# The square of a projection: read from PSUM, or from the copy in SBUF

## Chip, core and metric

The kernel runs on one core of one Trainium2 chip. The metric is the device time of one execution in microseconds (us). Engines: PE is TensorE (PEld its weight loads), DVE is VectorE, ACT is ScalarE, POOL is GpSimd, SP is SyncE, which only issues DMAs. "L303" is line 303 of the kernel.

## What is computed

The reference takes x of shape 4 x 512 x 128 and adds to it, in turn: half of a gated mixture of eight experts, a linear attention, the mixture again, half of a six-layer network, an attention with two key sets, and half of the six-layer network again. The change lies in the six-layer network, which therefore runs twice, 12 layers in all. The part of one layer that matters:

```python
q = l2norm(q) * qs
k = l2norm(k) * ksc
q = q * cos * scale + rotate_half(q) * sin * scale
k = k * cos * inv + rotate_half(k) * sin * inv
out = local_attention(q, k, v)      # 16 heads of 64, windows of 32, scores times 8, softmax
x = x + out @ Wo
x = x + ffn_layer(shift_tokens(x))  # layer norm, product gated by gelu
```

`l2norm` divides each head's vector by its length, so the sum of the squares of every k and q vector is needed. All of it is float32.

## The kernel before

**Units.** A layer is cut into 8 units: 4 batch rows b of 512 tokens, times 2 halves hf of 8 heads. A unit has 8 projections c (0 to 3 for k, 4 to 7 for q), each a 128 x 512 tile, features on the partitions. Over 12 layers these are 96 units and 768 projections.

**One projection** (`proj`) has five steps:
1. PE multiplies x with the weights in three passes (L274 to L276) into a PSUM bank `ps`, in the profile `qkps`, one of four banks that are shared with most other matmuls.
2. ACT copies it to SBUF, into a quarter of the tile `raw` (L300).
3. ACT squares it into `sq` (L303). PE sums the squares of the heads into `n2` (L321 for k, L355 for q).
4. DVE multiplies `ps` with the cosine table into `rtk` or `rtq` (L308).
5. POOL multiplies `raw` in place with the sine table (L310).

When four projections are through, `swap` (L389) issues two DMAs from POOL's queue that add the exchanged rows of `raw` onto `rtk` or `rtq`: this is the rotation.

**Lengths.** `norm` and `norm_q` turn the sums into reciprocal square roots with small operations of DVE (k: L327, L328, L335 to L342; q: L360, L362, L370 to L372) and of ACT (k: L330, L331, L345; q: L365, L366). For k, PE spreads them over the tile (`R`, L380) and DVE multiplies them in (L383). For q they enter the softmax.

**Attention.** `score` is PE (L419 the mask, L428). `soft` is DVE's maximum (L438) and difference (L440), POOL's product (L443), ACT's Exp (L445), DVE's sum (L448) and reciprocal (L450), POOL's product (L452) and DVE's transpose (L455). `vproj` (L401, copied by ACT at L407) gives values already multiplied with Wo, `out` (L471) and `add` (L478) put the result on x.

**Feed-forward**, once for each b and layer, in `Ffn`: two DMAs on SP's queue fetch the shifted half of x into `xs` (L601, L602); statistics on DVE (L607 to L612, L620 to L622), normalised on POOL (L626 to L628), gate, Gelu (L660, with two table loads), product (L671), output (L677).

**Order.** In the two runs of the six-layer network the order of instructions on each engine is written out: every step has a time in a table (`TIMES`), is held behind the steps that it needs, and all steps are sorted by that time and issued in this order. Each engine works through its own queue in order; waits between engines are put in by the framework from what each instruction reads and writes. In that order the square stands behind the copy and before DVE's product, and all steps of neighbouring units are interleaved. The preparation of weights (L182, L184 for the projections, L194 for the tables) and of x (`make_xT`, L259 to L269) lies among them.

The lines around the change:

```python
        nc.scalar.copy(raw, ps)
        yield
        self.sqs[c] = sq = tile_of(g, "t2", [128, 512], F32, "sq")
        nc.scalar.activation(sq, ps, AF.Square)
        yield
```

Of the kernel before, what the change touches and what calls it, by code (L numbers as in the profile page):

```python
# [9 lines left out]
AF = mybir.ActivationFunctionType  # L10
# [44 lines left out]
def tile_of(g, tag, shape, dt=F32, name=None, bufs=1):  # L55

    n = math.prod(shape[1:])
    e = 2 if dt == BF else 4
    size, bufs = SIZES.get(tag, (n * e, bufs))
    t = g.mem.tile([128, size // e], dt, tag=tag, name=name or tag, bufs=bufs)[0:shape[0], 0:n]  # L60
    if len(shape) > 2:
        d = "abcd"[:len(shape) - 1]
        t = t.rearrange("p (%s) -> p %s" % (" ".join(d), " ".join(d)), **dict(zip(d[1:], shape[2:])))
    return t
# [6 lines left out]
def bank(g, tag, shape=(128, 512), name=None):  # L71
    n = math.prod(shape[1:])
    t = g.psum.tile([128, 1024 if tag == "S" else 512], F32, tag=tag, name=name or tag, bufs=BANKS[tag])[0:shape[0], 0:n]
    if len(shape) > 2:
        d = "abcd"[:len(shape) - 1]
        t = t.rearrange("p (%s) -> p %s" % (" ".join(d), " ".join(d)), **dict(zip(d[1:], shape[2:])))
    return t
# [195 lines left out]
def mm3(nc, out, wh, wl, xh, xl):  # L273
    nc.tensor.matmul(out, lhsT=wh, rhs=xh, start=True, stop=False)  # L274
    nc.tensor.matmul(out, lhsT=wh, rhs=xl, start=False, stop=False)  # L275
    nc.tensor.matmul(out, lhsT=wl, rhs=xh, start=False, stop=True)  # L276


class Unit:
# [8 lines left out]
    def proj(self, c):  # L288
        g = self.g
        nc = g.nc  # L290
        xT = g.xT[(self.l, self.b)]
        s, i = c // 4, c % 4
        ps = bank(g, "mm", [128, 512], "qkps")
        W = g.wqk[(self.l, self.hf, c)]
        mm3(nc, ps, W[:, 0, :], W[:, 1, :], xT[:, 0, 0:512], xT[:, 1, 0:512])
        yield
        if i == 0:
            self.raw[s] = tile_of(g, "raw", [128, 4, 512], F32, "raw")
        raw = self.raw[s][:, i, :]
        nc.scalar.copy(raw, ps)  # L300
        yield
        self.sqs[c] = sq = tile_of(g, "t2", [128, 512], F32, "sq")
        nc.scalar.activation(sq, ps, AF.Square)  # L303
        yield
        if i == 0:
            self.rt[s] = tile_of(g, ("rtk", "rtq")[s], [128, 4, 512], F32)
        rot = g.rot[(self.l, s)]
        nc.vector.tensor_tensor(self.rt[s][:, i, :], ps, rot[:, 0, :], ALU.mult)  # L308
        yield
        nc.gpsimd.tensor_tensor(raw, raw, rot[:, 1, :], ALU.mult)  # L310
        yield
# [1047 lines left out]
```

## Time and profile before

| | |
|---|---|
| median of 3 runs | 4491.85 us (4482.15 to 4493.92) |
| the profiled execution's own time | 4486.91 us |
| its span, first to last instruction | 4485.1 us |
| mean granted TensorE clock | 0.939 |
| L300, copy, ACT | 768 times, 590 ns mean |
| L303, square, ACT | 768 times, 616 ns mean |
| L308, product with cosine, DVE | 768 times, 678 (k) and 684 ns (q) mean |
| L310, product with sine, POOL | 768 times, 1362 ns in the page's mean, median 1286 |
| swap (L389) | 384 DMAs of 512 KB, 6.5 to 6.7 us to landing |

Time is in us, the length of a single instruction in ns where marked. A group's line gives its busy time, the mean length of one, and the idle time of the engine just before it with what ended most of it. A line of the waits reads: who waited, for whom, total us, times, longest. The chain that ended last is followed back from the last instruction, at each step to what released it; its shares are of the span. In the timeline and the chain, times count from the start of the span.

### The profile page before, as it was taken

Reading aid. Unit: us, or ns where it says so; the run is one execution under the profiler, and the core shown is the slowest. Engines: PE = TensorE matmul, PEld = TensorE weight load, DVE = VectorE, ACT = ScalarE, POOL = GpSimd, SP = SyncE. Lnnn points to the kernel's source line nnn. Section 1 sums busy time; section 2 is a strip of 40 time slices with the busy share of each in tenths; the row PEclk is TensorE's granted clock in tenths of the full one; section 3 lists DMA queues with packets and bytes.
Section 4 is the critical chain, followed back from the end, with each engine's and each line's share of the span. In section 5 each row is a group of like instructions: output and inputs, shape, how many; then the busy total and the mean of one; then the engine's idle time right before and its main releaser. Section 6 shows DMA issues by size and latency. Waiting matters only on the chain.

```text
span 4485.1 us, 150251 instructions
## 1 busy us (share of the span) xinstructions
PE 3865.4 (86%) x66435; PEld 2663.9 (59%) x66436; DVE 3705.2 (83%) x6415; ACT 2604.5 (58%) x5050; POOL 2493.1 (56%) x2164
## 2 busy tenths in 40 slices
PE   8989978898888888988869998888889889888886
PEld 5666646666666666666533434566666666566665
DVE  6968978888898888888867776888888888888886
ACT  5434455665565565665536666555656656556563
POOL 4625656666666666666501112666666666666663
PEclk9999989999999999999979999999999999999998
DMA  2000033433434334343331222333343343433432
GB/s 61 19 10 15 22 86 74 90 70 81 88 66 91 71 76 88 70 88 73 84 95 49 69 76 52 70 80 82 72 86 73 78 90 61 89 69 77 85 62 49
DMA packets 163852, 312.44 MB, mean 70 GB/s; under 512 B 41304, under 2 KB 125664, under 8 KB 138176
## 3 DMA queue, kind: packets, MB, share of 16 engines
q0 software_dynamic: 31008, 202.40, 22.8%
q1 hardware_dynamic: 132192, 100.44, 7.8%
q8 instruction: 520, 8.52, 0.8%
q14 instruction: 132, 1.08, 0.1%
HBM read 77.49 MB, written 17.69 MB: 21 GB/s over the span
## 4 chain that ended last, share of the span: by engine, by line
DVE 38%; PE 37%; DMA 12%; issue 6%; ACT 4%; POOL 2%; SPq 1%; ACTq 0%; POOLq 0%; DVEq 0%
DMA xs<-x 10%; DVE sm L448 4%; PE vps L401 3%; DVE h L935 3%; DVE E L440 3%; PE S L428 3%; DVE mx L438 3%; DVE xT L269 3%; PE av L471 3%; DVE rtq L308 3%; PE S L1147 2%; DVE pt L455 2%; PE av L1184 2%; PE qkps L274 2%; PE ST L1176 2%
## 5 line engine op out<-in xcount | busy, mean ns | idle before, releaser
L310 POOL TENSOR_TENSOR raw<-raw,rot 128x512 f32<-128x512 f32 x768 | 1006.8, 1362 | 544.2 <-ACT raw L300 540.4
L300 ACT COPY raw<-qkps 128x512 f32<-128x512 f32 x768 | 453.3, 590 | 662.2 <-PE qkps L276 643.7
L401 PE MATMUL vps<-vo,xF 128*32 128x256 f32 x12288 | 751.6, 386 | 40.0 <-issue 29.3
L401 PEld LDWEIGHTS vps<-vo,xF 128*32 128x32 f32 x12288 | 405.9, 111 | 330.3 <-issue 81.6
L452 POOL TENSOR_TENSOR E<-E,smr 128x1024 f32<-128x1024 f32 x192 | 389.6, 2029 | 310.1 <-DVE smr L450 177.0
L407 ACT COPY vx<-vps 128x512 f32<-128x512 f32 x768 | 427.1, 584 | 108.6 <-PE vps L401 106.7
L303 ACT ACTIVATE sq<-qkps 128x512 f32<-128x512 f32 x768 | 473.1, 616 | 0.0
L443 POOL TENSOR_TENSOR E<-E,rq 128x1024 f32<-128x1024 f32 x192 | 388.8, 2025 | 95.6 <-DVE E L440 57.3
L471 PE MATMUL av<-vx,pt 128*32 128x128 f32 x11904 | 381.6, 275 | 58.1 <-DVE x L478 32.8
L274 PE MATMUL qkps<-xT,wqk 128*128 128x512 f32 x768 | 343.4, 447 | 73.3 <-DVE rtq L308 40.6
L471 PEld LDWEIGHTS av<-vx,pt 128*32 128x32 f32 x11904 | 335.7, 110 | 115.8 <-DVE x L478 49.3
L1148 DVE TENSOR_REDUCE nm<-S 128x1 f32<-128x512 f32 x512 | 325.2, 684 | 63.3 <-PE S L1147 62.7
L308 DVE TENSOR_TENSOR rtq<-qkps,rot 128x512 f32<-128x512 f32 x384 | 259.9, 684 | 134.2 <-ACT sq L303 132.6
L383 DVE TENSOR_TENSOR rtk<-rtk,R 128x512 f32<-128x512 f32 x384 | 254.0, 672 | 104.7 <-PE R L380 104.3
L677 PE MATMUL fout<-w,ge 128*128 128x128 f32 (+1 forms) x1152 | 231.9, 379 | 123.3 <-DVE rtk L383 120.4
L1177 ACT ACTIVATE E<-ST 128x512 f32<-128x512 f32 x512 | 273.8, 599 | 109.3 <-PE ST L1176 109.1
L937 POOL TENSOR_TENSOR h<-r,h 128x512 fp32r<-128x512 f32 x128 | 182.3, 1424 | 251.5 <-DVE h L935 237.9
L275 PE MATMUL qkps<-xT,wqk 128*128 128x512 f32 x768 | 310.9, 405 | 5.7 <-issue 2.9
L276 PE MATMUL qkps<-xT,wqk 128*128 128x512 f32 x768 | 309.4, 403 | 5.0 <-issue 5.0
L428 PE MATMUL S<-rtk,rtq 64*32 64x64 f32 (+1 forms) x24576 | 291.4, 229 | 15.5 <-issue 13.3
L428 PEld LDWEIGHTS S<-rtk,rtq 64*32 64x32 f32 x24576 | 284.1, 108 | 31.3 <-issue 18.1
L677 PEld LDWEIGHTS fout<-w,ge 128*128 128x128 f32 (+1 forms) x1152 | 218.4, 289 | 133.7 <-DVE rtk L383 129.4
(257 smaller groups left out, 8803.8 us busy)
## 6 DMA issues: line engine op xcount, KB each, us to landing
rtk<-raw POOLq DMA_DIRECT2D x192, 512.0 KB, 6.7
rtq<-raw POOLq DMA_DIRECT2D x192, 512.0 KB, 6.5
pd<-pc SPq DMA_DIRECT2D x36, 384.0 KB
wqkr<-in_L_ffn_Wqk SPq DMA_DIRECT2D x192, 64.0 KB
rot<-in_c_rot SPq DMA_DIRECT2D x24, 512.0 KB
k<-pd SPq DMA_DIRECT2D x32, 288.0 KB
r<-in_L_ffn_W SPq DMA_DIRECT2D x32, 256.0 KB
wvraw<-in_L_ffn_WvT SPq DMA_DIRECT2D x24, 256.0 KB
```

The costliest lines, as they stand in the source:

```text
L274: nc.tensor.matmul(out, lhsT=wh, rhs=xh, start=True, stop=False)
L300: nc.scalar.copy(raw, ps)
L303: nc.scalar.activation(sq, ps, AF.Square)
L308: nc.vector.tensor_tensor(self.rt[s][:, i, :], ps, rot[:, 0, :], ALU.mult)
L310: nc.gpsimd.tensor_tensor(raw, raw, rot[:, 1, :], ALU.mult)
L401: nc.tensor.matmul(ps[p * 32:(p + 1) * 32, ww, :], lhsT=xF[:, t0:t0 + 32], rhs=g.vo[(self.l, self.hf, p // 2)][:, p % 2, :], start=True, s ...
L407: nc.scalar.copy(self.v[th][:, 2 * t:2 * t + 2, :], ps)
L428: nc.tensor.matmul(self.S[k][p * 32:(p + 1) * 32, ab, w * 64 + 64 - n:w * 64 + 64], lhsT=self.rt[1][rows, p, t0:t0 + 32], rhs=self.rt[0][r ...
L443: nc.gpsimd.tensor_tensor(E4, E4, self.rq[:, :, 8 * k:8 * k + 8].unsqueeze(3).to_broadcast([128, 2, 8, 64]), ALU.mult)
L452: nc.gpsimd.tensor_tensor(E, E, r.unsqueeze(2).to_broadcast([128, 16, 64]), ALU.mult)
L471: g.nc.tensor.matmul(self.av[ww * 32:(ww + 1) * 32, k, :], lhsT=self.pt[w // 8][:, ab, w % 8, role, :], rhs=self.v[src // 8][:, src % 8, a ...
L677: nc.tensor.matmul(self.o[:, t, :], lhsT=h[0:k, t * 128:(t + 1) * 128], rhs=g.F[self.l].w2[0:k, i, :], start=(i == 0 and t == 0), stop=(i ...
```

## The change

The square's input is `raw`, the copy in SBUF, in place of `ps`, the bank in PSUM. Nothing else is touched: same engine, same size, same place in the order. The copy is written by the ACT instruction before it, and `raw` is later overwritten in place by L310.

```diff
         nc.scalar.copy(raw, ps)
         yield
         self.sqs[c] = sq = tile_of(g, "t2", [128, 512], F32, "sq")
-        nc.scalar.activation(sq, ps, AF.Square)
+        nc.scalar.activation(sq, raw, AF.Square)
         yield
```

## The prediction

> **What bounds the kernel.** I read the page first, for the busy shares and the chain that ended last; then the waits; then the users of the lines that the diff touches; then the chain and the timeline of a few stretches inside a feed-forward block.
>
> ```profile
> PE 3865.4 (86%) x66435; PEld 2663.9 (59%) x66436; DVE 3705.2 (83%) x6415; ACT 2604.5 (58%) x5050; POOL 2493.1 (56%) x2164
> ...
> DVE 38%; PE 37%; DMA 12%; issue 6%; ACT 4%; POOL 2%; SPq 1%; ACTq 0%; POOLq 0%; DVEq 0%
> ```
>
> No engine is full. The end is set by a chain that alternates between DVE and PE; ACT and POOL, which the diff loads, are 4% and 2% of it. So I ask what hangs on the changed line, L303, and on the POOL product L310 that overwrites the tile L303 will now read. From the list of waits, then from the view of L303 (who waited for it: total us, times):
>
> ```profile
> POOL raw L310 <- ACT raw L300: 540.4, 244, 24.4
> DVE rtq L308 <- ACT sq L303: 132.6, 153, 4.2
> DVE rtk L308 <- ACT sq L303: 29.6, 62, 4.1
> ```
>
> DVE's L308 waits 215 times for the square, whose result it does not use. Over all 768 projections L308 never starts sooner than 0.03 us after L303's end. Both read one PSUM bank, and the program orders them. POOL waits only for the copy, L300. One case, as the chain of waits tells it (start, us, what):
>
> ```profile
> 1061.88 0.59 ACT raw L300
> 1062.47 0.51 ACT sq L303
> 1063.00 0.69 DVE rtq L308
> 1063.69 1.14 DVE mx L438
> ```
>
> Copy, square, product, each released by the one before: 0.51 us of square stand in the chain. The timeline of the same stretch (start, us, engine, line; in brackets the idle time before) shows ACT and POOL:
>
> ```profile
> 1061.88 0.59 ACT L300 COPY raw<-qkps 128x512 f32<-128x512 f32 x1
> 1062.37 0.60 ACT L303 ACTIVATE sq<-qkps 128x512 f32<-128x512 f32 x1
> ...
> 1064.96 0.24 ACT L330 ACTIVATE ky<-kn 128x32 f32<-128x32 f32 x1
> 1065.23 0.23 ACT L331 ACTIVATE ky<-ky 128x32 f32<-128x32 f32 x1
> ```
>
> ```profile
> 1062.55 2.54 POOL L310 TENSOR_TENSOR raw<-raw,rot 128x512 f32<-128x512 f32 x2 [2.41 <-ACT raw L300]
> ```
>
> L303 starts 0.49 us after a copy that lasts 0.59: they overlap by 0.10. L331, which needs L330's result, starts 0.03 us after its end. L310 starts when the copy is through, beside the square.
>
> **Removed: DVE's wait for the square.** In 748 of 768 cases L303 follows L300 directly on ACT, and its end is 0.505 us after L300's (median). So L308 may start up to 0.505 us earlier. In the chain "ACT sq L303" has 83 pieces, 42.0 us. Of these 67 lead to L308; the rest to another copy (13) or other ACT work (3). For the 67 the gain is the smaller of 0.505 us and DVE's idle time before that L308: 30.4 us. How much is kept depends on what DVE waits for next. For 33 it is a POOL product that DVE itself releases (L452), or a sum on PE: 16.0 us, kept in full. For 24 it is PE's spread R (L380), which hangs on DVE as well as on ACT and PE: 9.7 us, between none and all; I take half, 4.9. For 10 it is the next square: 4.7 us, taken as lost. Sum -20.9; bounds -16.0 and -30.4. All 230 idle stretches of DVE before L308, cut in the same way, are 87.8 us; that is the limit if nothing but DVE counted.
>
> **Added on ACT.** L303 now needs L300's result: it starts about 0.03 us after L300's end (as L331 does) instead of 0.10 before it. Its length from SBUF is between its own 0.606 and 0.622 (the 128x512 cast from SBUF, L811, which takes 0.580 from PSUM); I take 0.62. Its end comes 0.65 us after L300's, not 0.505: +0.145 us, and over 748 pairs 108 us more of an engine that has 1880 us idle. On the path: 16 pieces of the chain where more ACT work follows, 2.3 us, and DVE's 30 waits for the Gelu (L671, 39.4 us), at most 4.4 us. Sum between +2.3 and +6.7; I take +4. The rest is covered by slack: the sum of the exponentials (L448) starts 1.18 us or more after its Exp ended in 95% of cases. A page differs a little here: the Trainium skill, "ScalarE: Activation LUTs", section "What ACT_TABLE_LOAD costs", gives back-to-back ACTIVATEs an overlap of 93 ns where these rows show 0.10 to 0.11 us; losing it would make the ACT sum 93 us (748 times 0.093 plus 0.031), an estimate from that page, against 108 from the rows.
>
> **Added on POOL.** L310 must not overwrite what the square still reads, so its release moves from L300's end to L303's, 0.65 us later. Behind it in POOL's queue stand the swap DMAs (L389), the two softmax products (L443, L452) and the layer norm (L626). Moving L310 alone and letting the queue's idle time absorb it, 572 of the 768 start later, by 0.54 us on average; 125 swaps by 0.30 (38 us), 56 of L443 by 0.29 (16 us), 23 of L626 by 0.53 (12 us), almost none of L452. I cost this at nothing, because: the q swap lands 4.6 us or more before the first score in 95% of cases, the k swap 21.8 us or more; L443 is followed by the Exp, whose slack is the 1.18 us above; L628 behind L626 waits for DVE in any case. Without that cover it is the 66 us just listed.
>
> **Moved: L310 against DVE's small operations.** From the timeline of DVE, and of POOL beside it:
>
> ```profile
> 1081.78 1.08 DVE L370 TENSOR_TENSOR qr<-qy 128x32 f32<-128x32 f32 x1
> 1082.89 1.19 DVE L371 SCALAR_TENSOR_TENSOR qr<-qr,qn 128x32 f32<-128x32 f32 x1
> 1084.12 0.19 DVE L372 SCALAR_TENSOR_TENSOR rq<-qr,qy 128x32 f32<-128x32 f32 x1
> ```
>
> ```profile
> 1081.54 2.49 POOL L310 TENSOR_TENSOR raw<-raw,rot 128x512 f32<-128x512 f32 x2 [1.13 <-ACT raw L300]
> ```
>
> L370 takes 0.18 us elsewhere. Here it begins 0.24 us after an L310 and ends with it, and L371 ends with the second. In the chain 96 pieces are held by an L310 in this way (L328, L184, L370, L371, L612), for 59.9 us. If each hold grew by the 0.54 us of L310's delay, this would be +52 us. If instead what comes first goes first, 38 of the 96 arrive before L310's new start and pass, 44 wait longer, and the net is -21.6 us; operations newly caught, mostly L372 and L184, give back 9 to 26. I take -4, the middle of -12 and +5, and keep +52 as the far end. The rule behind the milder reading: the Trainium skill, "SBUF — State Buffer", section "SBUF: two separate sides", has VectorE and GpSimd share a port pair as a lock that whichever starts first keeps for its whole instruction. It speaks against this change too, since a later L310 meets other DVE work; by it the term is the -4, by the plain reading of the rows the +52.
>
> **Sum.** -20.9 + 4 - 4 = -21 us. The profiled execution took 4486.91 us (span 4485.1 and 1.8 around it), 4.9 below the median of the three runs, 4491.85. The sum gives 4466 by the first and 4471 by the second; I give 4471, as a median is what will be compared.
>
> **Rivals.**
> - *L310, later, holds DVE longer (slower).* Place: L328, L184, L370, L371 and L612, in each of 48 block passes. Price: +52 - 20.9 + 4 = +35 us, 4527. It cancels the gain when the holds grow by 17 us in sum, and decides beyond. For it: 59.9 us of holds already in the chain, with L310 as holder. Against it: L370 arrives only 0.12 to 0.32 us after L310, less than the 0.54 by which L310 moves.
> - *The gain is absorbed (no change).* The chain holds 31 landings of xs, each 11 to 15 us; what DVE saves just before a landing is lost, and where the k swap (L389, 45 waits for L308) starts sooner it shares the DMA engines with xs: L602 lasts 6.14 us at its shortest and 7.13 as a rule, so up to 1 us for each of the 38 waits on xs. If half of these lost 1 us, +19 - 21: about 4490.
> - *The change doesn't do what it says:* L308 stays behind the square by another tie. Neither its inputs (the bank, rot) nor its output names one. Then only ACT's +4 to +7 and POOL's delay remain: 4495 to 4500.
> - *ACT becomes late everywhere.* +108 us in its queue, but with 42% idle and the slack above I keep it inside the range, not as a case.
>
> **How the numbers follow.** About 0.3%, 13.5 us, can be told from no change. Forecast 0.52 (0.48 of it faster by more than that, 0.04 within); held DVE 0.24 (0.22 slower, 0.02 within); absorbed 0.20 (0.12 within, 0.05 faster, 0.03 slower); not done 0.04 (0.03 slower, 0.01 within). Together 0.53, 0.19, 0.28. The forecast's own range is 4451 to 4480: from -30.4 - 12 + 2.3 to -16.0 + 4. The whole range begins lower, at 4440, since the runs before begin 10 us below their median, and reaches to 4505, over the absorbed case and a third of the held one.
>
> **What would show it.** Right: "DVE rtq L308 <- ACT sq L303" gone, replaced by shorter waits for L300; L303 starting just after L300's end, at 0.61 to 0.63 us; POOL's wait before L310 now for the square and longer; qr L370 below its mean of 0.71 us. Wrong: L328, L184 or L612 with longer means, more time in the chain under xs, or waits for Exp (L445) before L448.

## The result, and the profile after

The changed kernel takes 4522.98 us (median; 4515.39 to 4534.39), the kernel before 4487.03 us on the same chip (4477.91 to 4493.92): a ratio of 1.0085, 95% interval 1.0066 to 1.0104. It is slower, by some 36 us, where 21 us less was forecast; 4522.98 lies outside the range of 4440 to 4505. The profiled execution of the changed kernel took 4524.28 us, with a span of 4521.8 us (36.7 longer than before) and a mean granted TensorE clock of 0.928 (0.939 before).

The page of the changed kernel, engine totals and chain of the end:

```profile
PE 3881.4 (86%) x66435; PEld 2648.5 (59%) x66436; DVE 3625.8 (80%) x6415; ACT 2699.4 (60%) x5050; POOL 2491.8 (55%) x2164
...
DVE 38%; PE 32%; DMA 17%; issue 5%; ACT 5%; POOL 2%; SPq 0%; DVEq 0%; POOLq 0%; ACTq 0%
DMA xs<-x 15%; DVE sm L448 4%; PE vps L401 3%; DVE E L440 3%; DVE h L935 3%; DVE mx L438 3%; DVE xT L269 3%; DVE rtq L308 3%; PE S L1147 3%; DVE pt L455 3%; PE av L1184 3%; PE ST L1176 2%; PE S L428 2%; PE av L471 2%; PE qkps L274 2%
```

DVE was busy for 79 us less than before, and yet the end came later. In the chain the share of DMA went from 12% to 17%, all of the rise from the landing of `xs`, which was 10% of the span (427.6 us) and is 15% (678.8 us). The list of waits after the change (who waited for whom: total us, times, longest):

```profile
POOL raw L310 <- ACT sq L303: 596.9, 304, 25.0
...
DVE bst L609 <- DMA xs<-x: 305.2, 48, 9.2
...
DVE rtq L308 <- ACT raw L300: 78.9, 121, 4.2
```

and two lines of the same list of the kernel before:

```profile
POOL rtk L389 <- DVE rtk L308: 119.4, 45, 2.9
...
DVE bst L609 <- DMA xs<-x: 98.7, 38, 8.7
```

DVE's wait for the square is gone, and L308 now waits for the copy alone, as forecast. The new cost is in the second line: L609, the first statistics of the feed-forward block, waits for `xs` in all 48 passes, 305.2 us in place of 98.7. POOL's wait for L308 ahead of the k swap has nearly vanished (119.4 us before; 14.8 us, 11 times, after): the swap is issued sooner. The next step joins these two.

**One pass, after and before.** The timelines (start, length, engine, line; in brackets the idle time before). After:

```profile
1089.84 0.75 SPq L601 DMA_DIRECT2D xs<-x  x1
...
1090.29 0.18 DVE L370 TENSOR_TENSOR qr<-qy 128x32 f32<-128x32 f32 x1
1090.50 0.19 DVE L371 SCALAR_TENSOR_TENSOR qr<-qr,qn 128x32 f32<-128x32 f32 x1
...
1090.71 2.49 POOL L310 TENSOR_TENSOR raw<-raw,rot 128x512 f32<-128x512 f32 x2 [1.80 <-ACT sq L303]
1090.73 1.29 DVE L372 SCALAR_TENSOR_TENSOR rq<-qr,qy 128x32 f32<-128x32 f32 x1
...
1094.40 1.71 POOL L389 DMA_DIRECT2D rtk<-raw  x2 [1.20 <-DVE rtk L308]
...
1104.30 0.23 DVE L609 BATCH_NORM_STATS2 bst<-xs 128x6 f32<-128x64 f32 x1 [4.46 <-DMA xs<-x]
```

Before, the same place in the network (L310, L370 and L371 of this pass are shown in the prediction):

```profile
1081.34 0.75 SPq L601 DMA_DIRECT2D xs<-x  x1
...
1086.68 1.71 POOL L389 DMA_DIRECT2D rtk<-raw  x2 [2.65 <-DVE rtk L308]
...
1092.79 0.20 DVE L609 BATCH_NORM_STATS2 bst<-xs 128x6 f32<-128x64 f32 x1
```

Count from the issue of `xs` (L601). Before, L310 began at +0.20, just ahead of L370, and held L370 and L371 for 1.08 and 1.19 us. After, it begins at +0.87; L370 and L371 went through at 0.18 and 0.19 us, and only L372 is caught. DVE is that much sooner through its queue, so L308 of the last k projection is sooner done, and the k swap that waits for it is issued at +4.56 in place of +5.34. In most passes the swap comes sooner still (+3.87, below), as POOL then finds L308 already done. Then L609 starts at +14.46 in place of +11.45: DVE, which was ready sooner, waits 4.46 us for a transfer that lands 3 us later.

**Why the transfer lands later.** `xs` comes as 511 packets of 256 B on SP's queue (508 of L601, 3 of L602). The packet records of these two passes, and of the next pass of the changed kernel:

| start of packet, from the issue of `xs` | 100th | 450th | 490th | 495th | 500th | 508th |
|---|---|---|---|---|---|---|
| before | +3.13 | +8.10 | +8.66 | +8.74 | +8.80 | +8.92 |
| after | +3.14 | +8.11 | +8.67 | +9.94 | +12.51 | +13.89 |
| after, the next pass (swap at +3.87) | +3.61 | +13.52 | +14.08 | +14.15 | +14.22 | +14.34 |

In the first two rows nothing differs up to the 490th packet, at 71 in a us. The swap's packets, 8 KB and about 0.64 us each, begin at +6.8 before and at +6.0 after. They leave `xs` alone for more than 2 us; then `xs` all but stands, with single packets between theirs, until the swap's are through. Before, all but three packets of `xs` were through by then; after, some twenty were left.

The first pass shown after is one of ten of the milder kind, with the swap at +4.55 or +4.56. In 34 of the 46 passes it is issued at +3.86 to +3.93, as in the third row: there the standstill begins at about +8.0, after 386 to 440 packets, with 71 to 125 left. Either way ten packets get through in 5.1 us, and what is left then goes at the old rate. A pass that is caught so loses some 5 us, with twenty packets left or with a hundred.

**All passes.** In 46 passes (the last of each run of layers left out), medians, in us after the issue of `xs`, with the mean where it is used below:

| | k swap issued | DVE ready for L609 | first L609 (mean) | rest of the pass, mean | pass, mean |
|---|---|---|---|---|---|
| before | 5.54 | 12.19 | 13.60 (13.58) | 55.49 | 69.07 |
| after | 3.88 | 8.77 | 14.83 (14.83) | 54.96 | 69.79 |

Over the 48 passes the stretch from issue to L609 grew by 57.6 us in sum, and the rest shrank by 24.5; with 4.3 more ahead of the first pass this makes 37.4, close to the 36.7 us of the span.

### The profile page after: what moved, and what is told of

It is laid out like the page before. It is cut to its first block, busy times and chain, and to the rows that moved or that the text cites. A ratio compares the mean times of both kernels' runs of the same rounds, so it can differ in the third digit from the quotient of the medians.

```text
span 4521.8 us, 150253 instructions
## 1 busy us (share of the span) xinstructions
PE 3881.4 (86%) x66435; PEld 2648.5 (59%) x66436; DVE 3625.8 (80%) x6415; ACT 2699.4 (60%) x5050; POOL 2491.8 (55%) x2164
## 4 chain that ended last, share of the span: by engine, by line
DVE 38%; PE 32%; DMA 17%; issue 5%; ACT 5%; POOL 2%; SPq 0%; DVEq 0%; POOLq 0%; ACTq 0%
DMA xs<-x 15%; DVE sm L448 4%; PE vps L401 3%; DVE E L440 3%; DVE h L935 3%; DVE mx L438 3%; DVE xT L269 3%; DVE rtq L308 3%; PE S L1147 3%; DVE pt L455 3%; PE av L1184 3%; PE ST L1176 2%; PE S L428 2%; PE av L471 2%; PE qkps L274 2%
## 5 line engine op out<-in xcount | busy, mean ns | idle before, releaser
L310 POOL TENSOR_TENSOR raw<-raw,rot 128x512 f32<-128x512 f32 x768 | 1003.5, 1356 | 599.3 <-ACT sq L303 596.9
L401 PE MATMUL vps<-vo,xF 128*32 128x256 f32 x12288 | 766.0, 392 | 39.1 <-issue 19.6
L300 ACT COPY raw<-qkps 128x512 f32<-128x512 f32 x768 | 443.7, 578 | 482.7 <-PE qkps L276 463.6
L274 PE MATMUL qkps<-xT,wqk 128*128 128x512 f32 x768 | 352.4, 459 | 209.9 <-DVE rtq L308 180.0
L303 ACT ACTIVATE sq<-raw 128x512 f32<-128x512 f32 x768 | 484.7, 631 | 23.6
L443 POOL TENSOR_TENSOR E<-E,rq 128x1024 f32<-128x1024 f32 x192 | 406.4, 2117 | 33.6 <-DVE rq L372 25.6
L274 PEld LDWEIGHTS qkps<-xT,wqk 128*128 128x128 f32 x768 | 151.5, 197 | 309.9 <-DVE rtq L308 201.8
L275 PE MATMUL qkps<-xT,wqk 128*128 128x512 f32 x768 | 318.6, 415 | 7.0 <-issue 3.5
L308 DVE TENSOR_TENSOR rtq<-qkps,rot 128x512 f32<-128x512 f32 x384 | 258.7, 685 | 80.2 <-ACT raw L300 78.9
L276 PE MATMUL qkps<-xT,wqk 128*128 128x512 f32 x768 | 317.2, 413 | 5.2 <-issue 5.2
L428 PEld LDWEIGHTS S<-rtk,rtq 64*32 64x32 f32 x24576 | 295.8, 112 | 24.6 <-issue 13.4
L428 PE MATMUL S<-rtk,rtq 64*32 64x64 f32 (+1 forms) x24576 | 302.5, 238 | 6.5 <-issue 5.1
L609 DVE BATCH_NORM_STATS2 bst<-xs 128x6 f32<-128x64 f32 x192 | 35.8, 186 | 305.2 <-DMA xs<-x 305.2
```

The source lines that it names most:

```text
L303: nc.scalar.activation(sq, raw, AF.Square)
L401: nc.tensor.matmul(ps[p * 32:(p + 1) * 32, ww, :], lhsT=xF[:, t0:t0 + 32], rhs=g.vo[(self.l, self.hf, p // 2)][:, p % 2, :], start=True, s ...
L428: nc.tensor.matmul(self.S[k][p * 32:(p + 1) * 32, ab, w * 64 + 64 - n:w * 64 + 64], lhsT=self.rt[1][rows, p, t0:t0 + 32], rhs=self.rt[0][r ...
L443: nc.gpsimd.tensor_tensor(E4, E4, self.rq[:, :, 8 * k:8 * k + 8].unsqueeze(3).to_broadcast([128, 2, 8, 64]), ALU.mult)
```

## The experiments

The theory (T1): the removed wait is worth what was forecast; the later L310 lets L370 and L371 pass, which pulls the k swap of every second unit into the packets of `xs`, and this costs more than all the gain. The rivals: the later L310 holds DVE longer in sum, or ACT, with its longer chain of copy and square, is late. Every ratio is to the kernel before on the same chip.

**The halves of the change: b_order and sq_other.** b_order is the kernel before with the square issued ahead of the copy, both from PSUM. L310 has to wait for the copy, now second, and L308 is no sooner: a later L310 alone, but for a square that is ready some 0.5 us sooner.

```diff
+        nc.scalar.activation(sq, ps, AF.Square)
+        yield
         nc.scalar.copy(raw, ps)
         yield
-        nc.scalar.activation(sq, ps, AF.Square)
-        yield
```

> The kernel before with the square issued ahead of the copy, both from PSUM: L310 is released by the end of the second of the two, about 0.5 us later than before, and DVE's L308 still waits for both. So this is the delay of L310 alone, without the sooner L308. Theory 1: L370 and L371 pass ahead of L310 (means near 0.2 us), the k swap starts about 4 us after the issue of xs instead of 5.5, the first L609 starts 14.4 us or later after it, and the time is 4520 to 4550 us. Theory 2: L370 and L371 may pass too, but the landing of xs does not move; 4490 to 4510.

Measured: 4533.5 us, 1.0113 (1.0093 to 1.0132). Its groups (busy us, mean ns, idle before) and waits:

```profile
L370 DVE TENSOR_TENSOR qr<-qy 128x32 f32<-128x32 f32 x96 | 21.6, 225 | 0.0
```

```profile
DVE bst L609 <- DMA xs<-x: 283.9, 48, 9.2
```

The later L310 alone brings the loss, more of it than the change does, with L370 free (0.225 us; 0.707 before) and the k swap at +3.75. Longer holds, the first rival, would need longer small operations. Some are longer (L328 has a mean of 0.431 us in place of 0.336), but in sum DVE is busy for less, 3617.9 us in place of 3705.2. A late ACT is out as well: the square still reads PSUM here, and ACT's busy time, 2604.3 us, is that of the kernel before (2604.5).

sq_other squares another tile of the same size in SBUF, which is ready early: L308 is freed from the square, and L310 waits for the copy as before. Left out are the lengths of q and k.

```diff
-        nc.scalar.activation(sq, ps, AF.Square)
+        nc.scalar.activation(sq, g.xF[(self.l, self.b)][:, 0:512], AF.Square)
```

> The changed kernel with the square reading another SBUF tile of the same size (xF, the unit's input) in place of raw; the lengths of q and k are thereby left out. L308 and L310 are both released by the copy: the sooner L308 alone, without the later L310. Theory 1: L370 stays held (mean near 0.7 us), the k swap starts 5.3 us or later after the issue of xs, xs lands as before, and the gain of the prediction shows: 4455 to 4475 us. Rival (the sooner L308 by itself starts the k swap sooner): the k swap starts 5 us or less after the issue, 4500 us or more.

Measured: 4461.03 us, 0.9952 (0.9936 to 0.9968), 20.6 us less than before.

```profile
DVE bst L609 <- DMA xs<-x: 120.4, 47, 8.7
```

The k swap is issued at +5.54 as before, the first L609 starts at +13.44 in the mean (13.58 before), and the wait for `xs` is near the old one. So the sooner L308 by itself does not move the swap. The two halves, -20.6 and +51.9, add up to +31, near the +36 of the change.

**The swap out of the way: a_move and b_move.** In the table of times the k swap of every second unit is put behind L630, after the statistics that read `xs`: a_move on the changed kernel, b_move on the kernel before.

```diff
-    ('swap', 1, 0): (-1.362,),
+    ('swap', 1, 0): (0.820,),
```

> The changed kernel, with the k swap (L389) of every second unit moved in POOL's queue behind the layer norm's products (L626 to L630), so that it starts after xs has landed. Theory 1 (the k swap, started 1.7 us sooner than before after the issue of xs, holds up the landing of xs in 46 passes): the first L609 starts about 10 to 11 us after the issue of xs instead of 14.8, DVE's waits for xs fall from 305 us to under 150, and the time falls below both kernels, to between 4400 and 4465 us. Theory 2 (the later L310 and the longer square cost the time themselves, and the wait for xs only shows slack): xs lands a little sooner, something else is late, 4510 to 4530 us.

> The kernel before, with the same k swap moved behind L630. Theory 1: xs, which before landed 12.3 to 15 us after its issue, lands at 10 to 11; DVE reaches L609 only about 12 us after the issue, since L370 and L371 are still held by L310, so the gain is smaller than in the changed kernel: 4430 to 4465 us. Theory 2: within 10 us of 4487.

Measured: a_move 4406.52 us, 0.9834 (0.981 to 0.9858), as T1 expected; the first L609 starts at +9.91 (median). b_move 4518.74 us, 1.0071 (1.0043 to 1.0098): a miss. There the stretch to L609 fell by 1.7 us a pass, since DVE, still held by L310, is ready at +11.75 and no sooner; and the rest of the pass grew by 2.4 us (55.49 to 57.93). That price, which a_move pays too (rest 57.73), I had left out. No wait for the swap's landing has grown. What has is ACT's wait for POOL's product L443, since the swap, 1.71 us on POOL, now stands a little ahead of L443. Before, then b_move:

```profile
ACT E L445 <- POOL E L443: 119.3, 113, 2.5
```

```profile
ACT E L445 <- POOL E L443: 222.4, 123, 4.1
```

This points to the swap's own time on POOL; how much of the 2.4 us it explains was not measured apart.

**A better place, on all four kernels.** With 0.795 in that entry the swap stands on POOL's queue behind the first product L310 of a q projection and the clearing of a column in the preparation of x (L262), at about the time of the statistics on `xs`. The edit is made to the kernel after (a_mid), before (b_mid), to b_order (border_mid) and to sq_other (sqother_mid, lengths of q and k left out again).

> The changed kernel with the k swap a little earlier in POOL's queue than behind L630: behind the first q product (L310) and L262, ahead of the next L310, so that it starts about 10.8 us after the issue of xs, just when xs has landed. If the landing of xs sets the pass and the 2.8 us by which the rest of the pass grew with the swap behind L630 come from its 1.7 us on POOL ahead of L310 and L443: xs lands at about 9.9 us as there, the rest of the pass goes back to 55 to 56 us, 4320 to 4390 us. If the growth of the rest has another source (PE, or the later k swap's landing): 4400 to 4420 us.

> The kernel before with the k swap at that same place. xs is there at 10 us, but DVE, held at L370 and L371, comes to L609 only 11.7 us after the issue: 11.8 + 55.7 us a pass, 4410 to 4450 us. If a later k swap costs by itself (as 4519 us with the swap behind L630 may say): 4480 to 4520 us.

> Square ahead of the copy, both from PSUM, and the k swap at that place: the later L310 alone, the collision with xs taken away. Theory: L370 and L371 pass ahead of L310, DVE is at L609 about 9 us after the issue, xs lands at 9.9; what is missing against the changed kernel with this swap is the sooner L308, 15 to 30 us: 4340 to 4415 us, and well below the kernel before with this swap. If the later L310 has no merit of its own: not below that one.

> The square from xF (the lengths of q and k are thereby left out), and the k swap at that place: the sooner L308 alone, L310 not delayed. Theory: L370 and L371 stay held, DVE is at L609 about 11 us after the issue; 15 to 30 us below the kernel before with this swap: 4390 to 4430 us, above the changed kernel with it. If the sooner L308 were the whole merit of the change: the same time as the changed kernel with this swap.

Measured, in us, with the ratio to the kernel before:

| | swap in its old place | swap moved |
|---|---|---|
| before | 4487 | 4450.4, 0.9923 (0.9896 to 0.9949) |
| L308 sooner alone (sq_other) | 4461.0, 0.9952 | 4430.6, 0.9887 (0.9856 to 0.9919) |
| L310 later alone (b_order) | 4533.5, 1.0113 | 4372.1, 0.975 (0.9723 to 0.9776) |
| both, the change | 4523.0, 1.0085 | 4360.6, 0.9726 (0.9702 to 0.9751) |

The sooner L308 is worth 21 and 20 us in the two columns. The later L310 costs some 50 us in the left column and gains 78 in the right: its sign hangs on where the k swap stands. On top of the sooner L308 the later L310 says the same, without the sooner square of b_order: 62 us lost on the left, 70 gained on the right. The two gains do not add up in full: on top of the later L310 (from b_order to the change, from border_mid to a_mid), the sooner L308 is worth about 11 in both columns, with ACT's longer chain included in the difference. b_mid came out 0.4 us above the expected 4450, sqother_mid 0.6 above its 4430; the other two lie inside. In a_mid, the waits and the timeline of the same pass:

```profile
DVE bst L609 <- DMA xs<-x: 85.8, 43, 8.7
```

```profile
1072.78 0.75 SPq L601 DMA_DIRECT2D xs<-x  x1
...
1073.64 2.49 POOL L310 TENSOR_TENSOR raw<-raw,rot 128x512 f32<-128x512 f32 x2 [1.79 <-ACT sq L303]
...
1082.94 0.20 DVE L609 BATCH_NORM_STATS2 bst<-xs 128x6 f32<-128x64 f32 x1
...
1084.34 1.71 POOL L389 DMA_DIRECT2D rtk<-raw  x2 [0.41 <-PE xTps L259]
```

L310 is as late as in the changed kernel, the swap comes behind L609, and L609 starts at +10.16 after the issue of `xs`. This version, the change with one time altered, is the fastest complete kernel here, 4360.56 us, and beats both.

**The dose: a_hold3 and a_hold6.** In the changed kernel POOL clears an unused 128x512 tile three or six times just ahead of this k swap, which only delays the swap and what is behind it on POOL.

```diff
+        if s == 0 and self.hf:
+            hold = tile_of(self.g, "hold", [128, 512], F32, "hold")
+            for _ in range(3):    # a_hold6: 6
+                self.g.nc.gpsimd.memset(hold, 0.0)
```

> The changed kernel, its queues in their order, with three POOL memsets of a 128x512 scratch tile (about 0.5 us each) directly ahead of the k swap of every second unit. The k swap should start 5.0 to 5.5 us after the issue of xs, instead of 3.9, about where it starts in the kernel before (5.5). Theory (what decides is whether the swap's data starts to flow before the last packets of xs): xs lands between 11 and 15 us after its issue, from pass to pass, as before; with DVE at L609 at about 9 us this gives 4440 to 4510 us, below the changed kernel in spite of 75 us more work on POOL. If it is the later place in the queue that gave the gain of the moved swap, and not the data: 4520 to 4550 us.

> The same with six memsets: the k swap starts 6.3 to 7 us after the issue of xs. Theory: the last packets of xs are through before the swap's data flows, xs lands at 10 to 11.5 us in nearly all passes, 4370 to 4430 us. Otherwise: 4530 us or more, as 150 us of POOL work are added.

Measured: a_hold3 4492.24 us, 1.0028 (1.0016 to 1.004); a_hold6 4384.79 us, 0.9789 (0.9765 to 0.9813). Six idle clears on POOL make the changed kernel faster by 138 us (4523.0 to 4384.8). The waits of a_hold3, then of a_hold6 (the four added lines make L609 L613; each pass has four of these operations):

```profile
DVE bst L613 <- DMA xs<-x: 270.9, 59, 9.6
```

```profile
DVE bst L613 <- DMA xs<-x: 142.3, 71, 8.7
```

With the swap at +3.88 (no hold) the first statistics start at +14.83 (median); at +5.19 (three) at +9.3 to +15.2 from pass to pass, mean 13.31; at +6.94 (six) at +9.95. The kernel before, with its swap at +5.54, stood in the same uncertain band.

**Without it: a_noswap.** The changed kernel without the two DMAs of this k swap; left out is that half of the rotation of k.

```diff
-        for d in range(2):
+        for d in range(0 if s == 0 and self.hf else 2):
```

> The changed kernel without the k swap of every second unit (half of the rotation of k is thereby left out in these units). Theory: xs lands at 9.3 to 10 us after its issue, and the time is near that of the swap put behind the landing of xs, 4330 to 4380 us. If the DMA traffic is not what holds xs: xs stays at 14.5 us or so, 4500 us or more.

Measured: 4326.47 us, 0.966 (0.9639 to 0.9681), a little below what was expected. The first L609 starts at +9.98, where a_mid and a_hold6 have it too (+9.92 and +9.95): so much `xs` takes by itself. What a_mid leaves on the table, 34 us, is in the rest of the pass (55.57 us here, 56.36 there, over 46 passes).

## Why the prediction was wrong

**The removed wait (-20.9): right.** "DVE rtq L308 <- ACT sq L303" is gone, and the half that holds only this term gave -20.6 us, with an interval that reaches from -14 to -29. That the two agree to 0.3 us is more than the interval can show. (The 0.505 us it starts from is the mean over all 768 projections; the median, as which it was given, is 0.500.)

**ACT (+4): the mechanism right, its place on the path not measured apart.** The view of L303 after the change (least, median and longest length in ns, then first and last start):

```profile
L303 ACT ACTIVATE sq<-raw x768: 614/631/639, 589.7 to 4446.3; 128x512 f32<-128x512 f32 x192
```

It starts 0.03 us after the copy's end, as L331 showed, and takes 0.631 us where 0.62 was taken. Where it directly follows the copy (741 times) its end comes 0.663 us after the copy's, 0.500 before: some 121 us in ACT's queue where 108 were forecast, 95 of it busy time. Nothing in the runs shows it late: the later L310 alone, without that longer ACT chain, cost more than the change.

**POOL's later release, "at nothing": failed.** The k swaps were put at 0.30 us later, by a model that moved L310 alone. In fact the 46 swaps are issued 1.66 us sooner (median), because what they wait for, DVE's L308, is sooner, with L370 and L371 no longer held ahead of it. And the cover I named, that the swap lands 21.8 us before the first score, answers the wrong question. It guards against a late swap; nothing guarded `xs` against an early one.

**L310 against DVE's small operations (-4): the step that failed.** That L370 passes was forecast, and it did; so was that L372 and L184 are caught. What was wrong is the worth of it, and that its worth was taken to be only the sum of the holds. (L370 also arrives sooner than the 0.12 to 0.32 us after L310 that the prediction gave: of 45 held ones 33 start 0.04 us behind an L310 and 11 at 0.17 to 0.25. That is still less than the 0.54 by which L310 moves.) From the groups before the change:

```profile
L370 DVE TENSOR_TENSOR qr<-qy 128x32 f32<-128x32 f32 x96 | 67.9, 707 | 0.0
...
L371 DVE SCALAR_TENSOR_TENSOR qr<-qr,qn 128x32 f32<-128x32 f32 x96 | 62.1, 647 | 3.3
...
L328 DVE TENSOR_SCALAR kn<-kt 128x32 f32<-128x32 f32 x96 | 32.3, 336 | 3.3
...
L372 DVE SCALAR_TENSOR_TENSOR rq<-qr,qy 128x32 f32<-128x32 f32 x96 | 18.4, 192 | 3.3
```

and after it:

```profile
L328 DVE TENSOR_SCALAR kn<-kt 128x32 f32<-128x32 f32 x96 | 50.7, 528 | 3.3
...
L372 DVE SCALAR_TENSOR_TENSOR rq<-qr,qy 128x32 f32<-128x32 f32 x96 | 29.4, 307 | 3.3
...
L370 DVE TENSOR_TENSOR qr<-qy 128x32 f32<-128x32 f32 x96 | 21.8, 227 | 0.2 <-ACT qy L366 0.2
...
L371 DVE SCALAR_TENSOR_TENSOR qr<-qr,qn 128x32 f32<-128x32 f32 x96 | 18.4, 192 | 3.3
```

L370 and L371 gave back 46 and 44 us of DVE (96 times 0.480 and 0.455) and L612 9; L328, L184 and L372 took 18, 16 and 11. Where the swap is out of the way the later L310 is worth 78 us, far past the -12 of my bounds; where it is not, it costs some 50, in 5 us standstills of `xs`. I summed the holds and stopped. The question of what DVE releases next when it is faster, and what that meets, was put only as a rival. The far end, +52, happens to be the size of the loss, but its reason, longer holds, is refuted by L370's own row.

**The rival "L310, later, holds DVE longer" (4527): the right number for a wrong reason,** as b_order shows. Three of the signs set down for it did come: longer means of L328 (0.336 to 0.528 us) and L184 (0.598 to 0.683), and more of the chain under `xs`. L612 fell (0.357 to 0.170 us), and so did the holds in sum; signs that two causes share did not tell them apart.

**The rival "the gain is absorbed" (about 4490): the right mechanism, mis-sized.** It named the k swap, sooner by L308, on the DMA engines beside `xs`; what makes it sooner is the later L310, for with L308 freed alone (sq_other) it stays at +5.54. Its price came from the spread of L602's own length, 6.14 to 7.13 us, at most 1 us a wait, lost in half of the 38: 19 us. The measured price against the kernel before is 57.6 us over 48 passes, and against a landing left alone some 5 us a pass (14.83 to 9.92). Without the collision the change is worth -90 us (the right column), with it +36. It should have been read from the landings of `xs` themselves: in the kernel before they were already 11 to 15 us (two of the 31 about 9), a spread that I quoted and did not ask about. The packet records of before show the edge. With the swap at +5.34 to +5.41 (11 passes) the last packet of `xs` is through by +11.5. With the swap at +5.53 to +5.58 (33 passes) it is through at +11.2 to +11.9 in nine and at +13.2 to +14.7 in 24. So the swap's issue alone does not sort them; how far `xs` has got by then nearly does. Its 100th packet starts at +3.0 to +3.2 in the 11, at +3.48 to +3.70 in the nine, and at +3.66 or later in the 24.

## What to carry to other kernels

When an edit makes an engine faster, follow what that engine releases, transfers above all, and list what is in flight at the new time; a cover of "it lands early enough" says nothing about what an earlier start disturbs. Where a landing time has two values in the profile of before, find what separates them before any saving is counted, since a shift of a microsecond there can outweigh the whole edit. And once it is found, take the collision away: here one time in the order's table turned a loss of 36 us into a gain of 125.

## What the runs showed of the hardware

A transfer of small packets was not slowed evenly by a large one beside it; it ran, stood, and ran again. `xs` moved at 70 to 71 packets of 256 B in a us with and without the swap. In the changed kernel its standstill began 2.6 to 2.9 us after the swap's first 8 KB packet (2.2 in one pass of the 46). In the 36 passes with more than 30 packets left by then, ten came through in 5.10 to 5.15 us, and the rest at 68 to 70 in a us. In the third row of the packet table the ones from the 411th on came 0.62, 0.64, 0.64 and 0.64 us apart, the length of one 8 KB packet of the swap (median 0.636). So the price is about 5 us, whether twenty packets are left or a hundred, and none if `xs` is through in time. An estimate from these numbers fits: a swap is 128 packets of 8 KB, 8 for each of the 16 DMA engines if they share evenly, and 8 times 0.636 is 5.1 us, as long as `xs` would have to share one engine with it. That `xs` is on one engine is not shown. The Trainium skill, "DMA: Bandwidth & Descriptors", section "Queues, rings and completion order", has each DMA engine take turns between its queues a whole packet at a time; these gaps agree with it, though the records do not say which engine carried which packet, nor whether the profile's packet is the page's.

SP's queue is held too: L602, the issue of the last piece of `xs`, is 7.13 us long in the median before, 7.12 in a_mid, and 10.21 after the change (6.8 to 6.9 in its ten milder passes).

The rule on the shared lock, cited in the prediction, holds in these rows: L370, which starts 0.42 us ahead of an L310, takes 0.18 us, and L372, which starts 0.02 us behind it, takes 1.29.
